# GpSimd multiplies two of the rows that VectorE adds: a two-layer graph attention kernel, layer 1

## The chip, the core and the metric

The kernel runs on 1 core of one Trainium2 chip. The metric is the device time of one execution in microseconds (us), the median of several runs. Engines are named as in the profile: PE is TensorE (PEld its weight loads), DVE is VectorE, ACT is ScalarE, POOL is GpSimd, SP is SyncE.

## The reference, cut to what matters

A graph of 10,000 nodes with 170,000 directed edges (80,000 random ones in both directions and a loop at each node). Two graph attention layers with a residual product, each followed by layer norms. Layer 1 has 4 heads of 256 columns, so a row of it has 1024; layer 2 has one head of 768.

```python
def gat_conv(x, edge_index, W, a_src, a_dst, bias, heads, out_ch, concat):
    ...
    xl = (x @ W).reshape(n, heads, out_ch)
    alpha_src = jnp.einsum('nhc,hc->nh', xl, a_src)
    alpha_dst = jnp.einsum('nhc,hc->nh', xl, a_dst)
    e = jax.nn.leaky_relu(alpha_src[src] + alpha_dst[dst], 0.2)
    m = jax.ops.segment_max(e, dst, num_segments=n)
    e = jnp.exp(e - m[dst])
    s = jax.ops.segment_sum(e, dst, num_segments=n)
    alpha = e / (s[dst] + 1e-16)
    msg = xl[src] * alpha[:, :, None]
    out = jax.ops.segment_sum(msg, dst, num_segments=n)
    ...
h = gat_conv(x, edge_index, W1, a_src1, a_dst1, b1, HEADS, HID, True)
h = jax.nn.relu(layer_norm(h, g1, be1)) + (h0 @ Wr1 + br1)
h1 = h
h = gat_conv(h, edge_index, W2, a_src2, a_dst2, b2, 1, OUT_DIM, False)
h = layer_norm(h, g2, be2) + (h1 @ Wr2 + br2)
x = _layernorm(x + h)
```

## The kernel before, in words

There are three parts. First (up to about 740 us) all rows `x @ W1` are computed and written to a table in HBM, each with its logit parts behind its 1024 columns, while the edges are sorted. Then layer 1 (about 766 to 3080 us) and layer 2 (to the end) go over 79 tiles of 128 nodes. The nodes are sorted by the number of their edges, so that a tile needs `SLOTS[t]` rows, one for each edge of its node with the most edges. The order of the tiles, `TURNS`, lets the sizes of layer 1 rise from 7 to 41 rows and fall again to 9.

Row k of a tile is fetched by one indirect DMA, which GpSimd issues (L470): 128 partitions, each its own table row of 4132 bytes. The rows go into a ring of 31 places (`RING1`); `ring.fetch` asks for a row when the one 31 before it has been used, so each gather waits for whoever used that place last.

The weighted sum over a tile's rows is shared between three engines by row:

- The first `on_pe(t)` rows: ScalarE multiplies the row in its place by the weights, one ACTIVATE for each of 4 heads (L558), and TensorE adds it up with an identity matmul (L931), for tile t + 1 while tile t is under way. The sum is the accumulator in PSUM.
- "Weighed" rows (`weighed(t)` of them, spread over the tile): VectorE multiplies and adds at once, four 128x256 instructions (L569).
- "Shared" rows (the rest): ScalarE multiplies (L558), VectorE adds one 128x1024 instruction (L565).

`PARTED` is 22: tiles with 22 rows or more are done in several parts, with a running maximum, and are not touched by the change. `FEW` is 11.

All engines work through their instructions in the order in which the program gives them. Within the loop over the rows k of tile t, `multiplied(k + 1 + LEAD)` puts ScalarE's multiplies four rows ahead of VectorE's add. At k = `soon - 2` (`soon` is n - 3, or n - 4 where the next tile has more than two rows on TensorE) GpSimd adds up the next tile's logits (L937 to L942); two rows later VectorE takes leaky ReLU and maximum (L194, L950, L953), ScalarE the exponent (L954), and a row after that VectorE divides by the sum (L974 to L976), after which ScalarE can begin with the next tile's rows. The last add of a tile is followed by the normalisation on VectorE (L580, L582, L594, L596, L1084), whose standard deviation comes from ScalarE (L584, L585). TensorE multiplies the tile's x by Wr1 (L177) and the normalised rows by W2 (L1156). SP issues the stores of x, of h1 and of layer 2's table row.

Of the kernel before, what the change touches and what calls it, by code (L numbers as in the profile page):

```python
# [32 lines left out]
OP = mybir.AluOpType  # L33
# [23 lines left out]
PARTED = 22  # L57
FEW = 11
# [26 lines left out]
def gnn_kernel(ctx, tc, x, x_cols, src, dst, src_col, dst_col, W1, a_src1, a_dst1, b1, g1, be1, Wr1, br1,  # L85
               W2, a_src2, a_dst2, b2, g2, be2, Wr2, br2, out, n_edges):
    nc = tc.nc
    N, D0 = out.shape
    H1, DH1 = a_src1.shape
# [10 lines left out]
    SLOTS = CAPS  # L100
# [3 lines left out]
    FIRST, TOTAL = [0] * NT, 0  # L104
# [449 lines left out]
    def multiply(row, e, dh):  # L554

        for h in range(e.shape[1]):
            s = slice(h * dh, (h + 1) * dh)
            nc.scalar.activation(row[:, s], row[:, s], AF.Copy, scale=e[:, h:h + 1])  # L558

    def weigh(acc, row, e, dh, first=None, shared=False):  # L560


        if shared:
            c = e.shape[1] * dh
            nc.vector.tensor_add(acc[:, :c], acc[:, :c], row[:, :c])  # L565
            return
        for h in range(e.shape[1]):
            s = slice(h * dh, (h + 1) * dh)
            nc.vector.scalar_tensor_tensor(acc[:, s], row[:, s], e[:, h:h + 1],  # L569
                                           (acc if first is None else first)[:, s], op0=OP.mult, op1=OP.add)  # L570
# [41 lines left out]
    with tc.tile_pool(name="w1", bufs=1) as w1p, tc.tile_pool(name="l1", bufs=2) as io, \  # L612
# [63 lines left out]
        def new_row():  # L676
            return io.tile([P, R1], F32, name="row", bufs=4)
# [57 lines left out]
        for t in range(NT % 2):  # L735
            xT, row = xTs.pop(t), new_row()
# [94 lines left out]
    SLOTS, FIRST = [SLOTS[t] for t in TURNS], [FIRST[t] for t in TURNS]  # L831
# [35 lines left out]
    def ordered_layer1(mem):  # L867
        nc.scalar.add_instruction(mybir.InstLoadActFuncSet(name=nc.get_next_instruction_name(), act_func_set_id=6, engine=nc.scalar.engine))
        with tc.tile_pool(name="b1", bufs=1) as pool, tc.tile_pool(name="small1", bufs=2) as small, \
# [3 lines left out]
            ring = Ring(table1, RING1, {}, [mem.rearrange("p (k n) -> p k n", n=R1)])  # L873
# [35 lines left out]

            accs = [ps_acc.tile([P, 2 * BANK], F32, name=f"acc{i}") for i in range(2)]  # L910

            def on_pe(t):


                n = SLOTS[t]
                if n <= FEW + 1:
                    return int(n > FEW)
                return min((n - FEW) // 2 + (n > 18 and n % 2 == 0), ON_PE1)

            def later_on_pe(t):  # L920

                return min(max((SLOTS[t] - 20) // 2, 1), ON_PE1 - 2)
# [34 lines left out]
            def weights_of(t):  # L957

                n, m, at = SLOTS[t], on_pe(t), FIRST[t]
                cuts = cuts_of(t)  # L960
                ad = ring.slot(at)[:, C1:C1 + H1]
# [53 lines left out]
            def cuts_of(t):  # L1015

                n = SLOTS[t]
                groups = 1 if n < PARTED else -(-2 * n // ring.size)
                size = 8 if groups == 2 else (n - 5) // groups
                return [0] + [n - size * g for g in range(groups - 1, -1, -1)]  # L1020

            def by_vector(t, k):
                lo = max(c for c in cuts_of(t)[:-1] if c <= k)
                return k - lo >= (later_on_pe(t) if lo else on_pe(t))

            def weighed(t):

                return sum(SLOTS[t] >= n for n in (0, 0, 17, 19))

            def shared(t, k):  # L1030
                i = k - on_pe(t)
                if len(cuts_of(t)) > 2:
                    return by_vector(t, k) and i % (SHARE - 1) > 0
                w = weighed(t)
                return by_vector(t, k) and i * w % (SLOTS[t] - on_pe(t)) >= w

            last = None
            full = None
# [29 lines left out]
            for t in range(NT + 1):  # L1068
                live, events = t < NT, []
                n = SLOTS[t] if live else 0  # L1070
                first = done = on_pe(t) if live else 0
                cuts = cuts_of(t) if live else []
                moves = []

                def started():

                    r_before, means = last
                    return r_before, means, deviation(small, pieces(means[:, :C1], BANK))

                def normalised(r_before, means, stats):  # L1080

                    h = pool.tile([P, C1], F32, name="h")
                    scaled(h, [means[:, :C1]], stats, g1_b, be1_b)
                    nc.vector.scalar_tensor_tensor(h, h, 0.0, r_before[:, :C1], op0=OP.max, op1=OP.add)  # L1084
                    return h

                early = live and last and not ready
                if early:
# [6 lines left out]
                    h, moves = normalised(*started()), []  # L1095
# [6 lines left out]
                def row_of(k):  # L1102
                    lo = max(c for c in es if c <= k)
                    return es[lo][0][:, k - lo], es[lo][1] if k == lo else None

                def multiplied(upto):
                    nonlocal done
                    while done < min(upto, n):
                        if shared(t, done):
                            multiply(ring.slot(FIRST[t] + done), row_of(done)[0], DH1)  # L1110
                        done += 1

# [13 lines left out]
                if live and t and not early and not turned:  # L1126
                    xT, moves = from_x(t)
                turned, turn = [], live and 0 < t < NT - 1 and len(cuts) == 2
                multiplied(first + 2)
                if last and not early:  # L1130
                    h = normalised(*norm)
                if not live:
                    begun = next(begin)
                for move in moves:
                    move()
                multiplied(first + LEAD)
                if last:
                    hT = pool.tile([P, K1, P], F32, name="hT")
# [39 lines left out]
                def due(k):  # L1178
                    while events and events[0][0] <= k:
                        events.pop(0)[1]()  # L1180
# [10 lines left out]
                for k in range(n):  # L1191
                    if k + 3 * LEAD + 2 in cuts[1:-1]:
                        next(later)
                    if k + 2 * LEAD + 2 in cuts[1:-1]:
                        next(later)
                    if k + 2 * LEAD in cuts[1:-1]:
                        lo, es_lo = next(later)
                        es[lo] = es_lo
                    multiplied(k + 1 + LEAD)
                    if k == soon - 2:  # L1200
                        next(ahead, None)
                    if soon <= k < soon + 2:
                        ready += itertools.islice(ahead, 1)
                    if k + 2 in cuts[1:-1]:
                        next(later)
                    weights, fade = row_of(k)
                    if fade is not None:
                        for h in range(H1):
                            s = slice(h * DH1, (h + 1) * DH1)
                            nc.vector.scalar_tensor_tensor(acc[:, s], acc[:, s], fade[:, h:h + 1], ring.slot(FIRST[t] + k)[:, s],  # L1210
                                                           op0=OP.mult, op1=OP.add)
                    if not k and by_vector(t, k):
                        for h in range(H1):
                            s = slice(h * DH1, (h + 1) * DH1)
                            nc.vector.tensor_scalar(acc[:, s], ring.slot(FIRST[t])[:, s], weights[:, h:h + 1], None,
                                                    op0=OP.mult)
                    elif by_vector(t, k):
                        weigh(acc, ring.slot(FIRST[t] + k), weights, DH1, shared=shared(t, k))
                    if t:
                        ring.fetch(min(FIRST[t] + k + 1 + ring.size, upto[t][k >= soon - 2] if t in upto else TOTAL))  # L1220
                    due(k)
# [453 lines left out]
    with tc.If(all_fits > 0) as fit:  # L1675
        with tc.tile_pool(name="rows", bufs=1) as rows_pool:
            mem = rows_pool.tile([P, RING1 * R1], F32, name="ring")
            ordered_layer2(mem, ordered_layer1(mem))
# [49 lines left out]
```

## Time and profile before

| | us |
|---|---|
| median of 3 runs | 4923.9 (4920.7 to 4933.22) |
| profiled execution | 4928.81, span 4926.9 |

| Engine | busy us | share of the span |
|---|---|---|
| PE | 4379.8 | 89% |
| DVE | 4216.4 | 86% |
| ACT | 3291.0 | 67% |
| POOL | 3444.1 | 70% |

The profile is one execution, taken by the hardware profiler. A row of a group gives line, engine, operation, what is written and read, count, busy time, the mean in ns of one instruction, and the idle time of the engine before them with what ended it; "issue" stands for idle time in which the engine waited for nothing that the profile shows. A row in order of time gives start, length, engine, line and operation; like instructions that follow each other are merged with their count. Busy time of PE is modelled, and each matmul of 512 columns stands as two records.

### The profile page before, as it was taken

The page shows a single profiled execution, that of the slowest core. Times are in us where ns is not written, and L with a number is a line of the kernel's source. Part 1 is how long each engine was busy: PE and PEld are TensorE (multiplying, and loading weights), DVE is VectorE, ACT ScalarE, POOL GpSimd, SP SyncE. Part 2 cuts the span into 40 slices and gives each one's busy share as a digit, 9 for nine tenths or more (in the row PEclk, how much of TensorE's full clock was granted, in tenths as well). Part 3 has the DMA queues.
Part 4 walks back from the last instruction along what each step waited for, and adds up shares of the span by engine and source line. Part 5 has one row for each costly group of instructions (what it writes and reads, how often), then busy time and mean ns, then how long its engine had stood idle before and what let it go on. Part 6 is the DMA issues. An engine that isn't in the chain of part 4 may idle for free. (4 is left out here: it accounts for less than half of the span.)

```text
span 4926.9 us, 52519 instructions
## 1 busy us (share of the span) xinstructions
PE 4379.8 (89%) x12262; PEld 2264.3 (46%) x12262; DVE 4216.4 (86%) x5935; ACT 3291.0 (67%) x8969; POOL 3444.1 (70%) x3722
## 2 busy tenths in 40 slices
PE   9999998999999997899999999788787887787884
PEld 4443444554545543445444545444444444444442
DVE  7887897899999998898999998588887888888887
ACT  5753445899999998889999987344444444444443
POOL 6876766666777777777776664477777777777774
PEclk9999999999999999999999999889898898998987
DMA  4323438999999998999999996799999999999996
GB/s 162 124 104 129 103 108 330 352 359 370 379 378 391 401 384 296 361 370 389 389 376 375 368 356 244 285 369 372 360 375 369 369 369 366 370 368 365 370 367 224
DMA packets 433415, 1588.03 MB, mean 322 GB/s; under 512 B 77207, under 2 KB 82135, under 8 KB 433094
## 3 DMA queue, kind: packets, MB, share of 16 engines
q0 software_dynamic: 321040, 1283.72, 70.3%
q1 hardware_dynamic: 99490, 269.38, 14.6%
q10 hardware_dynamic: 12564, 31.47, 2.0%
q8 instruction: 101, 1.65, 0.1%
q14 instruction: 220, 1.80, 0.1%
HBM read 1426.26 MB, written 177.29 MB: 325 GB/s over the span
## 5 line engine op out<-in xcount | busy, mean ns | idle before, releaser
L470 POOL DMA_INDIRECT ring<-table,slots x2663 | 2646.9, 994 | 1123.5 <-issue 366.7
L558 ACT ACTIVATE ring<-ring,e 128x256 f32<-128x256 f32 x4468 | 1823.4, 502 | 71.8 <-DVE e L976 51.7
L569 DVE SCALAR_TENSOR_TENSOR acc<-ring,e,acc 128x256 f32<-128x256 f32 (+1 forms) x1915 | 1426.3, 745 | 81.0 <-PE acc L931 25.2
L565 DVE TENSOR_TENSOR acc<-acc,ring 128x1024 f32<-128x1024 f32 x869 | 1069.9, 1231 | 70.7 <-ACT ring L558 12.1
L1156 PE MATMUL half<-w,hT 128*128 128x512 f32 (+1 forms) x2528 | 841.2, 486 | 0.0
L177 PE MATMUL big<-wr,xT 128*128 128x512 f32 x1896 | 829.4, 594 | 0.5 <-ACT xT L892 0.5
L1348 PE MATMUL big<-wr,w 128*128 128x512 f32 (+1 forms) x2464 | 810.6, 487 | 13.6 <-ACT w L1354 12.5
L1156 PEld LDWEIGHTS half<-w,hT 128*128 128x128 f32 x2528 | 472.8, 189 | 341.6 <-issue 295.4
L1348 PEld LDWEIGHTS big<-wr,w 128*128 128x128 f32 x2464 | 468.6, 190 | 344.2 <-issue 298.6
L177 PEld LDWEIGHTS big<-wr,xT 128*128 128x128 f32 x1896 | 355.2, 191 | 417.9 <-issue 417.1
L931 PE MATMUL acc<-ring,ident 128*128 128x512 f32 x992 | 460.1, 612 | 71.1 <-ACT ring L558 50.4
L1314 PE MATMUL sums<-ring,diagonals 128*128 128x512 f32 x740 | 304.3, 569 | 182.9 <-ACT diagonals L1311 167.9
L1314 PE MATMUL sums<-ring,w 128*128 128x512 f32 x736 | 291.3, 553 | 172.4 <-ACT w L1311 172.4
L541 ACT ACTIVATE e<-e,least 128x19 f32<-128x19 f32 (+14 forms) x82 | 25.3, 308 | 614.1 <-DVE least L537 592.3
L690 ACT ACTIVATE scr<-scr 128x256 f32<-128x256 f32 x624 | 250.5, 403 | 160.5 <-DVE scr L683 156.3
L931 PEld LDWEIGHTS acc<-ring,ident 128*128 128x128 f32 x992 | 187.8, 194 | 305.6 <-issue 145.8
L1314 PEld LDWEIGHTS sums<-ring,diagonals 128*128 128x128 f32 x740 | 161.8, 223 | 320.7 <-ACT diagonals L1311 193.6
L630 PE MATMUL one<-wr,mixed 128*128 128x512 f32 x702 | 307.6, 592 | 0.0
L1314 PEld LDWEIGHTS sums<-ring,w 128*128 128x128 f32 x736 | 157.4, 218 | 302.0 <-ACT w L1311 183.3
L695 POOL TENSOR_TENSOR row<-row,none 128x1024 f32<-128x1024 f32 x69 | 168.2, 2438 | 115.1 <-DVE scr L683 45.7
L1362 ACT ACTIVATE spare<-acc 128x768 f32<-128x768 f32 x158 | 126.8, 802 | 167.6 <-DVE acc L1376 92.6
L630 PE MATMUL one<-w,xT 128*128 128x512 f32 x492 | 227.0, 598 | 10.8 <-DMA w<-in_W_dram 5.6
(236 smaller groups left out, 4697.7 us busy)
## 6 DMA issues: line engine op xcount, KB each, us to landing
ring<-table,slots POOLq DMA_INDIRECT x2663, 6.6
h_d<-hT SPq DMA_DIRECT2D x79, 512.0 KB, 8.5
table<-row SPq DMA_DIRECT2D x78, 516.0 KB, 3.2
w<-h_d SPq DMA_DIRECT2D x77, 512.0 KB, 8.5
table<-row SPq DMA_DIRECT2D x79, 385.0 KB, 6.3
ring<-table SPq DMA_DIRECT2D x79, 385.0 KB, 6.5
w<-x_d SPq DMA_DIRECT2D x79, 384.0 KB, 6.8
x_d<-xt SPq DMA_DIRECT2D x77, 384.0 KB, 6.4
```

Source lines behind the costliest of these rows:

```text
L177: nc.tensor.matmul(p[:, c:e], aT[:, j, :], w[:, j, c:e], start=(j == 0), stop=(j == k - 1))
L470: nc.gpsimd.indirect_dma_start(out=to, out_offset=None, in_=table, in_offset=bass.IndirectOffsetOnAxis(ap=index, axis=0), **more)
L558: nc.scalar.activation(row[:, s], row[:, s], AF.Copy, scale=e[:, h:h + 1])
L565: nc.vector.tensor_add(acc[:, :c], acc[:, :c], row[:, :c])
L569: nc.vector.scalar_tensor_tensor(acc[:, s], row[:, s], e[:, h:h + 1], (acc if first is None else first)[:, s], op0=OP.mult, op1=OP.add)
L630: nc.tensor.matmul(p, aT[:, j, :], w[:, j, :], start=(start and j == 0), stop=(j == k - 1), skip_group_check=True)
L690: nc.scalar.activation(m[:, s], m[:, s], AF.Copy, accum_out=row[:, C1 + i * H1 + h:C1 + i * H1 + h + 1])
L695: engine.tensor_add(row[:, lo:hi], row[:, lo:hi], b1_b[:, lo:hi])
L931: nc.tensor.matmul(acc[:, c:c + BANK], ident, ring.slot(q + k)[:, c:c + BANK], start=(k == 0), stop=(k == m - 1))
L1156: nc.tensor.matmul(q, hT[:, j, :], w2[:, j, c:c + q.shape[1]], start=(j == 0), stop=(j == K1 - 1))
L1314: nc.tensor.matmul(to[:, c:d], diagonal, ring.slot(at + k)[:, c:d], start=(k == n - m), stop=(k == n - 1))
L1348: nc.tensor.matmul(r[:, c:d], hT[:, j, :], wr2[:, j, c:d], start=(j == 0), stop=(j == K1 - 1))
```

## The change

Tiles of layer 1 with 13 to 21 rows (`helped`; the first tile of the order is left out) share their rows in another way. Of each, the last two shared rows are multiplied by GpSimd, four instructions of 128x256 a row, in place in the ring, and not by ScalarE. They stand in GpSimd's queue ahead of the gathers that belong to rows 1 and 3 of the tile. VectorE adds these rows as it adds the other shared ones. VectorE weighs no row at 13 to 16 rows (two before), one at 17 and 18 (three before), two at 19 to 21 (four before). TensorE sums (n - 12) // 2 rows, at least one, which is one fewer than before at 15, 17, 19, 20 and 21 rows.

```diff
+            def helped(t):
+
+                return 0 < t and FEW + 2 <= SLOTS[t] < PARTED
+
             def on_pe(t):
                 n = SLOTS[t]
+                if helped(t):
+                    return max((n - FEW - 1) // 2, 1)
                 if n <= FEW + 1:
                     return int(n > FEW)
                 return min((n - FEW) // 2 + (n > 18 and n % 2 == 0), ON_PE1)
...
             def weighed(t):
 
-                return sum(SLOTS[t] >= n for n in (0, 0, 17, 19))
+                return sum(SLOTS[t] >= n for n in ((17, 19) if helped(t) else (0, 0, 17, 19)))
...
+            def by_pool(t):
+
+                return [k for k in range(SLOTS[t]) if shared(t, k)][-2:] if helped(t) else []
...
                 cuts = cuts_of(t) if live else []
+                given = by_pool(t) if live else []
...
                     while done < min(upto, n):
-                        if shared(t, done):
+                        if shared(t, done) and done not in given:
                             multiply(ring.slot(FIRST[t] + done), row_of(done)[0], DH1)
                         done += 1
...
                     multiplied(k + 1 + LEAD)
+                    if k in (1, 3) and given:
+                        row, weights = ring.slot(FIRST[t] + given[k // 2]), row_of(given[k // 2])[0]
+                        for h in range(H1):
+                            s = slice(h * DH1, (h + 1) * DH1)
+                            nc.gpsimd.tensor_scalar(row[:, s], row[:, s], weights[:, h:h + 1], None, op0=OP.mult)
                     if k == soon - 2:
                         next(ahead, None)
```

## The prediction

> **What bounds the kernel now.** First the page (span, the engines' busy times, the costliest groups), then the busy times per stretch, then the order of time inside two tiles.
>
> ```profile
> span 4926.9 us, 52519 instructions
> PE 4379.8 (89%) x12262; PEld 2264.3 (46%) x12262; DVE 4216.4 (86%) x5935; ACT 3291.0 (67%) x8969; POOL 3444.1 (70%) x3722
> L470 POOL DMA_INDIRECT ring<-table,slots x2663 | 2646.9, 994 | 1123.5 <-issue 366.7
> L565 DVE TENSOR_TENSOR acc<-acc,ring 128x1024 f32<-128x1024 f32 x869 | 1069.9, 1231 | 70.7 <-ACT ring L558 12.1
> ```
>
> The whole-run shares hide what counts. Layer 1's tiles of 13 to 21 rows stand twice in the run, on a rising and a falling flank. The rows below are the falling flank, one stretch for each size from 21 down to 13 (2, 3, 3, 4, 3, 4, 4, 3 and 2 tiles), each cut at the last normalising step (L1084). Columns: stretch, its length, then busy time (and instructions) of PE, PEld, DVE, ACT, POOL, the granted clock, DMA share, GB/s.
>
> ```profile
> 2198.80:2265.20 66.40, 64.18 (x190) 32.42 (x189) 58.34 (x80) 61.56 (x158) 48.54 (x60) 1.00 1.00 376
> 2265.20:2356.80 91.60, 91.60 (x269) 47.03 (x268) 83.44 (x118) 87.75 (x225) 68.70 (x81) 1.00 1.02 401
> 2356.80:2446.10 89.30, 86.22 (x255) 44.13 (x254) 83.13 (x117) 81.25 (x208) 64.48 (x76) 1.00 1.02 389
> 2446.10:2562.80 116.70, 110.13 (x324) 56.27 (x323) 108.14 (x145) 109.53 (x281) 83.02 (x101) 0.99 1.00 377
> 2562.80:2647.80 85.00, 83.43 (x248) 42.58 (x247) 77.35 (x105) 76.37 (x196) 58.59 (x69) 1.00 1.01 382
> 2647.80:2757.70 109.90, 105.80 (x314) 54.24 (x313) 100.05 (x128) 103.24 (x266) 72.17 (x90) 0.98 0.98 363
> 2757.70:2860.30 102.60, 102.22 (x311) 53.41 (x309) 95.11 (x124) 95.33 (x245) 68.04 (x86) 1.00 0.99 372
> 2860.30:2936.50 76.20, 72.29 (x223) 38.16 (x222) 71.23 (x94) 68.59 (x175) 48.48 (x63) 1.00 0.97 352
> 2936.50:2985.60 49.10, 47.81 (x149) 25.51 (x148) 44.93 (x60) 42.27 (x108) 29.61 (x36) 1.00 0.98 354
> ```
>
> TensorE, VectorE and ScalarE are all between 86% and 100% here: three bounds lie within a few per cent of each other, so relief of one pays only up to the next. GpSimd looks free at 60 to 75%. It is not: its gathers do not follow one another without a gap. These are its rows at the end of a 20-row tile.
>
> ```profile
> 1608.33 0.99 POOL L470 DMA_INDIRECT ring<-table,slots  x1 [0.30 <-issue]
> 1609.32 0.12 POOL L937 MEMSET e<- 128x4 f32 x1
> 1609.39 0.36 POOL L939 TENSOR_TENSOR e<-ring 128x68 f32<-128x68 f32 x1
> 1611.69 1.07 POOL L470 DMA_INDIRECT ring<-table,slots  x1 [0.61 <-DVE e L953]
> 1615.73 0.99 POOL L470 DMA_INDIRECT ring<-table,slots  x1 [0.30 <-issue]
> 1621.11 1.85 POOL L470 DMA_INDIRECT ring<-table,slots  x1 [0.31 <-issue]
> ```
>
> A gather is 0.99 us long, but 0.30 us of idle time stands before each, also where it waits for nothing ("issue"): the pace is 1.29 us. A compute step follows a gather with no gap (1608.33 + 0.99 = 1609.32), and after the logits the gap is 0.61. So GpSimd's demand for a tile of n rows is its busy time, 0.30 for each of n + 1 gathers (one is x's), and 0.30 after the logits. For 20 rows: 68.70 / 3 = 22.9, plus 6.3, plus 0.3, makes 29.5 us of the 91.60 / 3 = 30.5 us that a tile takes. What is left over for GpSimd, by the same arithmetic, for 13 to 21 rows: 5.2, 4.4, 3.5, 4.0, 3.1, 2.4, 2.0, 1.0 and 2.0 us.
>
> **The change, part by part.** It touches 57 tiles (5, 6, 7, 8, 7, 8, 6, 6 and 4 of the sizes 13 to 21, layer 1 without its first turn). By the two helpers that count rows, VectorE weighs two rows fewer in each (114 rows). TensorE sums one row fewer at 15, 17, 19, 20 and 21 rows (30 tiles). VectorE adds two rows more at 13, 14, 16, 18 and three more at the others (144 rows). ScalarE multiplies as many rows as before: 30 fewer for TensorE, 144 more for VectorE, 114 given to GpSimd. GpSimd gets 2 x 4 multiplies of 128x256 a tile, 456 in all. No transfer, no SP instruction and no ScalarE queue entry is moved past another kind; the multiplies are put into GpSimd's queue ahead of the gathers of rows 1 and 3.
>
> The prices of VectorE and ScalarE come from a 15-row tile, ScalarE first, in order of time (start, length):
>
> ```profile
> 2807.51 4.90 ACT L558 ACTIVATE ring<-ring,e 128x256 f32<-128x256 f32 x12
> 2812.30 0.57 ACT L892 COPY hT<-half 128x512 f32<-128x512 f32 x1
> 2812.77 1.71 ACT L558 ACTIVATE ring<-ring,e 128x256 f32<-128x256 f32 x4
> 2814.84 11.28 ACT L558 ACTIVATE ring<-ring,e 128x256 f32<-128x256 f32 x28
> 2826.36 0.25 ACT L954 ACTIVATE e<-e 128x60 f32<-128x60 f32 x1 [0.24 <-DVE e L953]
> 2820.72 2.06 DVE L569 SCALAR_TENSOR_TENSOR acc<-ring,e,acc 128x256 f32<-128x256 f32 x4
> 2822.87 2.56 DVE L565 TENSOR_TENSOR acc<-acc,ring 128x1024 f32<-128x1024 f32 x2
> 2825.50 0.22 DVE L194 SCALAR_TENSOR_TENSOR e<-e 128x60 f32<-128x60 f32 x1
> 2826.18 1.22 DVE L565 TENSOR_TENSOR acc<-acc,ring 128x1024 f32<-128x1024 f32 x1
> 2827.96 2.49 DVE L565 TENSOR_TENSOR acc<-acc,ring 128x1024 f32<-128x1024 f32 x2
> 2830.49 0.70 DVE L580 BATCH_NORM_STATS2 st<-acc 128x6 f32<-128x512 f32 x1
> ```
>
> - VectorE: a weighed row takes 2822.87 - 2820.72 = 2.15 us, an added one (2825.50 - 2822.87) / 2 = 1.31. Two weighed for two added saves 1.7 us a tile, two for three saves 0.4.
> - TensorE: one row is four of the matmuls at L931, whose pace I take from the 24 of a tile's product at L177, 10.46 / 24 = 0.43 us (quoted below), so 1.7 us less in 30 tiles.
> - ScalarE: 1.61 us a row (11.28 for 7). This is slower than VectorE's add. Until now each weighed row, which needs no ScalarE, let it catch up; now two of these are gone and its rows end earlier in the tile, with GpSimd's two behind them. For 15 rows: today ScalarE does 11 of VectorE's rows from 2807.51 on; it will do 12, and 2807.51 + 12 x 1.61 + 0.93 (two hT copies) = 2827.8. VectorE then adds row 11 (ready 2826.2), does the logit steps (0.68, from 2825.50 to 2826.18), and starts row 12 at 2828.2 instead of 2826.18. Behind it stand the same three adds and the normalisation. That is +2.0 to +2.1 us although VectorE has less to do. The same subtraction gives 0, +1.0, +0.7 and +0.2 at 13, 14, 16 and 17. At 18 to 21, where ScalarE has more rows' lead and VectorE or TensorE held the end, it gives -1.2, -0.2, -0.8 and -0.6. Over the 57 tiles this is about +10 us: without any GpSimd cost the change is a wash.
> - GpSimd's multiply is not in the trace. The nearest rows:
>
> ```profile
> L702 POOL TENSOR_TENSOR mixed<-xT 128x384 f32<-128x384 f32 x20 | 22.2, 1110 | 0.5 <-PE one L630 0.5
> L695 POOL TENSOR_TENSOR row<-row,none 128x1024 f32<-128x1024 f32 x69 | 168.2, 2438 | 115.1 <-DVE scr L683 45.7 <-issue 30.6 <-DVE have L416 24.0
> L941 POOL TENSOR_SCALAR slots<-ring 128x2 int32<-128x2 f32 x4 | 1.1, 262 | 0.3
> L941 POOL TENSOR_SCALAR slots<-ring 128x18 int32<-128x18 f32 x5 | 1.6, 323 | 0.4
> L942 POOL MEMSET ring<- 128x25 f32 x12 | 1.5, 123 | 0.7
> L942 POOL MEMSET ring<- 128x90 f32 x5 | 0.9, 183 | 0.3
> 2811.35 10.46 PE L177 MATMUL big<-wr,xT 128*128 128x512 f32 x24
> ```
>
> A two-operand step grows by (2438 - 1110) / 640 = 2.08 ns an element; with one tensor operand I take half, 1.04, on the fixed 0.26 us of the small tensor-scalar: 0.26 + 256 x 1.04 ns = 0.53 us, so 8 x 0.53 = 4.2 us a tile. Low end: a memset, which reads nothing, carried on to 256 columns by its own slope, 0.183 + 166 x (183 - 123) / 65 ns = 0.34 us, 2.7 us a tile. High end: the small tensor-scalar's own slope, (323 - 262) / 16 = 3.8 ns, is from strided single elements and would give 1.2; the two-operand slope gives 0.79. I hold 0.34 to 0.85 for likely.
>
> The Trainium skill (GPSIMD Engine Reference, section 3.1) has a simple one-operand body at about 1.03 cycles an element of a 1.2 GHz clock; as an estimate that is 0.22 us on the same 0.26, 3.8 us a tile, and the sum below would be +77 instead of +90. No row here shows it.
>
> Sum for GpSimd: 4.2 us against the spare time above overruns by 0.7, 0.2, 1.1, 1.8, 2.3, 3.2 and 2.2 us at 15 to 21 rows; below 15 it fits. Per size the larger of this and ScalarE's tail holds, since both lie on one chain: gathers and multiplies, logits, VectorE's logit steps, weights, ScalarE's rows. 6 x 1.0 + 7 x 2.1 + 8 x 0.7 + 7 x 1.1 + 8 x 1.8 + 6 x 2.3 + 6 x 3.2 + 4 x 2.2 = **+90 us**.
>
> **Waits.** The multiply itself waits for little: its row has landed (the logits read it) and its weights are a tile's tail old. Behind it stand the gathers and then the next tile's logits at L939, for which VectorE's L194 waits; that wait should grow. The two rows' results are needed some ten adds (13 us) later, so VectorE does not wait for the multiply; were that cover gone, up to 2.1 us a row would show. The gathers start later, but GpSimd then sets the pace for their use too, so landing stays hidden.
>
> **Against the executions.** The profiled one took 4928.8 us (span 4926.9), 5 us above the median 4923.9. 4923.9 + 90 = **5014 us**.
>
> **Rivals.**
> 1. The aim is met: GpSimd and ScalarE's tail hide, and TensorE's idle time in the stretches at 13, 14, 16 and 18 rows (0.65, 1.3, 1.0, 1.6 us a tile) is what VectorE's 1.7 us can win, 32 us, plus 0.4 in 30 tiles: -44, **4880 us**. For it: VectorE is nearly full at 14 and 18 rows. Against: at 20 rows GpSimd has 1.0 us left, and eight fixed parts alone are 2.1. It decides if the multiply, in effect, costs under 0.2 us and ScalarE runs ahead of VectorE.
> 2. GpSimd's share is hidden, ScalarE's tail is not: +10, **4934 us**, no change. It needs the same small multiply.
> 3. A cheap multiply of 0.34 us: overruns only at 18 to 21 rows, 0.3, 0.7, 1.7 and 0.7: +47, **4971 us**.
> 4. A dear multiply, 0.73 to 0.85: the overrun reaches all sizes, +156 to +210, **5080 to 5134 us**.
> 5. A held port. The gather at 1621.11 took 1.85 us rather than 0.99, while VectorE ran the step below, two operands of which are in SBUF; VectorE's adds have the accumulator in PSUM.
>
> ```profile
> 1620.82 1.28 DVE L596 SCALAR_TENSOR_TENSOR h<-h,sd,norm 128x1024 f32<-128x1024 f32 x1
> ```
>
> If each tile's first multiply falls on this step, either waits: up to 0.86 us in 57 tiles, +49 on the sum, **5063 us**. The Trainium skill (SBUF — State Buffer, section Who interferes with whom) says such a VectorE step and a GpSimd step that reads SBUF exclude each other for a whole instruction; this gather agrees. By the section the adds would not be held.
>
> **How the numbers follow.** Chances: the forecast with a multiply of about 0.4 to 0.65 (4980 to 5050, its own range) 0.50; rival 5, 0.10; rival 4, 0.12; rival 3, 0.12; rival 2, 0.07; rival 1, 0.09. A measurement tells about 0.3%, 15 us, from no change. So faster 0.09, same 0.07, slower 0.84. From 4925 to 5110 the range takes in rivals 2, 3, 5 and most of 4 and leaves out rival 1 and the dearest multiplies, about 0.17.
>
> **What would show it.** In the profile of the changed kernel: a GpSimd tensor-scalar group, ring from ring, 456 times, near 0.53 us each; GpSimd's gathers at 18 to 21 rows all with the bare 0.30 before them; VectorE's L194 waiting for GpSimd's logits by 2 to 3 us a tile at those sizes, and its adds waiting for ScalarE's rows at 14 and 15; stretches of 20 rows near 33.7 us a tile and of 15 near 27.7. It is wrong if the multiply is near 0.2 us, if it runs beside the gathers' 0.30 gaps, or if ScalarE's rows are never late.

## The result, and the profile after

The changed kernel takes 5281.47 us (median of 6 runs), the kernel before 4929.47 us on the same chip (6 runs): a ratio of 1.0721, interval [1.071, 1.0732]. That is 352 us slower; 90 us were forecast. The profiled execution took 5287.69 us.

The page of the kernel after: span, busy times, and the groups that answer to those quoted of before (line, engine, operation, tile, count, then busy us and mean ns of one, then idle time ahead of it and what ended it). The edit moved L939 to L945, L954 to L960 and L931 to L937; L194, L470, L558, L565 and L596 kept their numbers.

```profile
span 5285.8 us, 52439 instructions
PE 4445.5 (84%) x12142; PEld 2287.2 (43%) x12142; DVE 4173.6 (79%) x5623; ACT 3293.7 (62%) x8969; POOL 3861.7 (73%) x4178
L565 DVE TENSOR_TENSOR acc<-acc,ring 128x1024 f32<-128x1024 f32 x1013 | 1247.3, 1231 | 145.8 <-ACT ring L558 77.0
L1215 POOL TENSOR_SCALAR ring<-ring,e 128x256 f32<-128x256 f32 x456 | 424.8, 945 | 4.5
L194 DVE SCALAR_TENSOR_TENSOR e<-e 128x56 f32<-128x56 f32 (+25 forms) x174 | 34.8, 200 | 352.9 <-POOL e L945 349.6
L960 ACT ACTIVATE e<-e 128x56 f32<-128x56 f32 (+12 forms) x92 | 23.2, 252 | 430.3 <-DVE e L959 423.2
```

The multiply (L1215) has a mean of 945 ns, not 530. VectorE's busy time fell by 43 us, as meant; its share fell by more than that because the span grew. The idle time in L194's row says why: VectorE now stands idle for 349.6 us ahead of its logit step, until GpSimd's logits (L945) are there. Before, this was 45.7 us:

```profile
L194 DVE SCALAR_TENSOR_TENSOR e<-e 128x56 f32<-128x56 f32 (+25 forms) x174 | 34.5, 198 | 49.9 <-POOL e L939 45.7 <-DVE e L533 0.2
```

So this wait grew by 304 us, most of the 352 us lost; counted in the 57 changed tiles alone, it grew from 10 to 317 us. ScalarE's exponent (L960) waits behind it.

The stretches of the falling flank, again cut at the last normalising step, for 21, 20, 16 and 15 rows (2, 3, 4 and 4 tiles; columns as in the prediction):

```profile
2379.90:2457.40 77.50, 61.69 (x170) 30.92 (x171) 57.80 (x70) 61.51 (x157) 63.31 (x75) 0.91 0.88 320
2457.40:2568.90 111.50, 90.68 (x251) 44.79 (x250) 83.13 (x102) 86.15 (x221) 89.52 (x104) 0.93 0.89 326
...
2933.40:3071.40 138.00, 112.48 (x314) 56.55 (x312) 94.64 (x105) 101.95 (x262) 102.69 (x123) 0.90 0.82 294
3071.40:3194.30 122.90, 104.07 (x296) 53.26 (x296) 94.16 (x105) 97.40 (x249) 100.00 (x120) 0.94 0.86 309
```

No engine's busy time fills a stretch any longer: at 20 rows GpSimd has the second most, 89.52 of 111.50 us, behind PE's 90.68. Its rows in time show that it is nonetheless the bound there. One 20-row tile, from the last gathers of the tile before to the logits; the fence begins and ends with VectorE's steps beside it:

```profile
1741.99 1.32 DVE L596 SCALAR_TENSOR_TENSOR h<-h,sd,norm 128x1024 f32<-128x1024 f32 x1 [0.39 <-ACT sd L585]
1741.38 0.99 POOL L470 DMA_INDIRECT ring<-table,slots  x1 [0.30 <-issue]
1742.41 4.41 POOL L1215 TENSOR_SCALAR ring<-ring,e 128x256 f32<-128x256 f32 x4
1746.99 1.06 POOL L470 DMA_INDIRECT ring<-table,slots  x1 [0.17 <-issue]
1748.35 1.01 POOL L470 DMA_INDIRECT ring<-table,slots  x1 [0.30 <-issue]
1749.40 3.64 POOL L1215 TENSOR_SCALAR ring<-ring,e 128x256 f32<-128x256 f32 x4
1753.20 1.06 POOL L470 DMA_INDIRECT ring<-table,slots  x1 [0.16 <-issue]
...
1768.59 0.36 POOL L945 TENSOR_TENSOR e<-ring 128x68 f32<-128x68 f32 x1
1769.77 0.24 DVE L194 SCALAR_TENSOR_TENSOR e<-e 128x80 f32<-128x80 f32 x1 [7.49 <-POOL e L945]
```

Nothing but the bare gap of the pace (about 0.3 us ahead of a gather) stands between GpSimd's steps, the logits come as late as its queue makes them, and VectorE waits 7.49 us. The first group of four meets L596 and takes 4.41 us instead of 3.64.

At 16 rows the queue is not full. One tile of that size:

```profile
2965.40 0.99 POOL L470 DMA_INDIRECT ring<-table,slots  x1 [0.30 <-DVE st L580]
2969.85 0.99 POOL L470 DMA_INDIRECT ring<-table,slots  x1 [3.46 <-ACT ring L558]
2970.89 3.65 POOL L1215 TENSOR_SCALAR ring<-ring,e 128x256 f32<-128x256 f32 x4
2974.71 1.06 POOL L470 DMA_INDIRECT ring<-table,slots  x1 [0.16 <-issue]
2976.07 1.02 POOL L470 DMA_INDIRECT ring<-table,slots  x1 [0.30 <-issue]
2977.12 3.63 POOL L1215 TENSOR_SCALAR ring<-ring,e 128x256 f32<-128x256 f32 x4
2980.92 1.06 POOL L470 DMA_INDIRECT ring<-table,slots  x1 [0.17 <-issue]
...
2992.49 0.34 POOL L945 TENSOR_TENSOR e<-ring 128x64 f32<-128x64 f32 x1
2992.87 0.23 DVE L194 SCALAR_TENSOR_TENSOR e<-e 128x64 f32<-128x64 f32 x1 [6.30 <-POOL e L945]
```

Here GpSimd waits 3.46 us at 2969.85 for the place of row 0 in the ring, and only then comes to the first multiply. From there to the logits there is no gap but the pace's. So part of what I had counted as spare lies ahead of the multiplies, where they cannot use it. The wait ends with one of ScalarE's multiplies (L558), and by the program these need the weights from the logits that GpSimd made in the tile before: the wait is a link of the loop of logits, weights, freed place, gather and logits again.

Mean time of a tile by size, both flanks, from one last normalising step to the next:

| Rows | 13 | 14 | 15 | 16 | 17 | 18 | 19 | 20 | 21 |
|---|---|---|---|---|---|---|---|---|---|
| before | 24.9 | 25.5 | 25.9 | 27.4 | 28.2 | 29.4 | 29.7 | 30.8 | 32.3 |
| after | 29.2 | 29.6 | 30.7 | 34.3 | 35.8 | 36.2 | 37.4 | 37.2 | 38.8 |
| more by | 4.3 | 4.1 | 4.8 | 6.9 | 7.6 | 6.8 | 7.7 | 6.4 | 6.5 |
| 7.5 less the spare time of the prediction | 2.3 | 3.1 | 4.0 | 3.5 | 4.4 | 5.1 | 5.5 | 6.5 | 5.5 |
| after: wait ahead of row 0's gather, above 0.30 | 1.8 | 0.4 | 0.7 | 3.2 | 3.5 | 2.3 | 1.9 | 0.0 | 0.0 |

The 57 tiles together went from 1602 to 1957 us, so all of the loss is in them (the tiles of 22 rows and more: 483 and 484 us). The fourth row is my own queue step with the measured price, 8 x 0.945 = 7.56 us, put as 7.5; over the 57 tiles it makes 252 us. At 20 rows, where the queue is full, it meets the measurement; at 16 and 17 rows it is 3 us short. The last row is the idle time, in the trace of after, ahead of the gather that precedes the first multiply. It makes 96 us over the 57 tiles, and the two rows together make 348 of the 355 us. This is a count of where GpSimd still idles; whether work could have used that time is tested by the run early. Between the first multiply and the next logits a gather stands idle longer than the pace's gap in only one of the 57 tiles, by 0.39 us.

### The profile page after: what moved, and what is told of

It is laid out like the page before. It is cut to its first block, busy times and chain, and to the rows that moved or that the text cites. A ratio compares the mean times of both kernels' runs of the same rounds, so it can differ in the third digit from the quotient of the medians.

```text
span 5285.8 us, 52439 instructions
## 1 busy us (share of the span) xinstructions
PE 4445.5 (84%) x12142; PEld 2287.2 (43%) x12142; DVE 4173.6 (79%) x5623; ACT 3293.7 (62%) x8969; POOL 3861.7 (73%) x4178
## 5 line engine op out<-in xcount | busy, mean ns | idle before, releaser
L470 POOL DMA_INDIRECT ring<-table,slots x2663 | 2636.9, 990 | 1060.2 <-issue 417.3
L558 ACT ACTIVATE ring<-ring,e 128x256 f32<-128x256 f32 x4468 | 1824.0, 501 | 78.3 <-DVE e L982 60.8
L565 DVE TENSOR_TENSOR acc<-acc,ring 128x1024 f32<-128x1024 f32 x1013 | 1247.3, 1231 | 145.8 <-ACT ring L558 77.0
L569 DVE SCALAR_TENSOR_TENSOR acc<-ring,e,acc 128x768 f32<-128x768 f32 (+1 forms) x1459 | 1203.4, 825 | 102.3 <-PE acc L937 60.9
L177 PE MATMUL big<-wr,xT 128*128 128x512 f32 x1896 | 850.4, 606 | 0.3 <-ACT xT L892 0.3
L937 PE MATMUL acc<-ring,ident 128*128 128x512 f32 x872 | 489.7, 717 | 310.8 <-ACT xT L892 211.9
L937 PEld LDWEIGHTS acc<-ring,ident 128*128 128x128 f32 x872 | 192.7, 230 | 570.8 <-ACT xT L892 228.5
L1215 POOL TENSOR_SCALAR ring<-ring,e 128x256 f32<-128x256 f32 x456 | 424.8, 945 | 4.5
L194 DVE SCALAR_TENSOR_TENSOR e<-e 128x56 f32<-128x56 f32 (+25 forms) x174 | 34.8, 200 | 352.9 <-POOL e L945 349.6
L960 ACT ACTIVATE e<-e 128x56 f32<-128x56 f32 (+12 forms) x92 | 23.2, 252 | 430.3 <-DVE e L959 423.2
```

The costliest lines, as they stand in the source:

```text
L177: nc.tensor.matmul(p[:, c:e], aT[:, j, :], w[:, j, c:e], start=(j == 0), stop=(j == k - 1))
L470: nc.gpsimd.indirect_dma_start(out=to, out_offset=None, in_=table, in_offset=bass.IndirectOffsetOnAxis(ap=index, axis=0), **more)
L937: nc.tensor.matmul(acc[:, c:c + BANK], ident, ring.slot(q + k)[:, c:c + BANK], start=(k == 0), stop=(k == m - 1))
L1215: nc.gpsimd.tensor_scalar(row[:, s], row[:, s], weights[:, h:h + 1], None, op0=OP.mult)
```

## The experiments

The kernels no_multiplies, multiplies_only, early, one_instruction, early_four and earlier_one ran on a chip on which the kernel before takes about 5412 us; the changed kernel itself was not run there. Ratios alone mislead here. That chip's extra time lies mostly in layer 2, which the change leaves alone: from the last normalising step of layer 1 to the end its traces take 2253 to 2264 us, those of before and after on the other chips 1827 and 1830. So the same loss in layer 1 is a smaller share of the whole there. The text therefore gives, beside each ratio, the time above before on the same chip, from the two medians; for the change it is 352 us. The tiles of layer 1 with fewer than 13 and more than 21 rows take 4 to 6% longer there too, so these differences may be off by some per cent.

**The change again**, beside kernels of the second group: 5279.48 us, ratio 1.0714 [1.0696, 1.0731].

> The changed kernel once more, as the measure for the others of this group on their chip: 1.072 of the time before by either theory.

That is 355 us above before. It is the yardstick for that group, and says that the result is steady.

**The price of the multiply by itself.** Groups of six GpSimd instructions behind the end of the before kernel's work (each loop is put on one line here):

```
+            a, b, unit = spare[:, :DH1], spare[:, DH1:2 * DH1], loops[:, 0:1]
+            for _ in range(6): nc.gpsimd.tensor_scalar(a, a, unit, None, op0=OP.mult)
+            for _ in range(6): nc.gpsimd.tensor_scalar(a, a, 1.0, None, op0=OP.mult)
+            for _ in range(6): nc.gpsimd.tensor_copy(a, b)
+            for _ in range(6): nc.gpsimd.tensor_tensor(a, a, b, op=OP.mult)
+            for _ in range(6): nc.gpsimd.tensor_tensor(a, b, unit.to_broadcast([P, DH1]), op=OP.mult)
+            for _ in range(6): nc.gpsimd.tensor_scalar(spare[:, :2 * DH1], spare[:, :2 * DH1], unit, None, op0=OP.mult)
+            for _ in range(6): nc.gpsimd.tensor_scalar(a[:, :P], a[:, :P], unit, None, op0=OP.mult)
```

> The kernel before with seven groups of six GpSimd instructions behind its last tile, where no other engine works: tensor-scalar by a per-partition operand 128x256, the same by a constant, copy, two-operand multiply, multiply by a spread column, tensor-scalar 128x512 and 128x128. Theory of the elements (about 3.4 ns each, whatever the second operand): per-partition and constant both 0.92 us, 512 columns 1.8, 128 columns 0.48. Theory of the operand (fetching the per-partition operand costs a fixed 0.4 us): constant 0.5, 512 columns 1.2, 128 columns 0.8.

Its groups on GpSimd (L1469 and L1471 are the 512 and 128 columns):

```profile
L1469 POOL TENSOR_SCALAR spare<-spare,loops 128x512 f32<-128x512 f32 x6 | 9.4, 1562 | 0.6
L1459 POOL TENSOR_SCALAR spare<-spare,loops 128x256 f32<-128x256 f32 x6 | 5.6, 932 | 0.5
L1461 POOL TENSOR_SCALAR spare<-spare 128x256 f32<-128x256 f32 x6 | 5.1, 847 | 0.5
L1465 POOL TENSOR_TENSOR spare<-spare 128x256 f32<-128x256 f32 x6 | 4.3, 722 | 0.5
L1467 POOL TENSOR_TENSOR spare<-spare,loops 128x256 f32<-128x256 f32 x6 | 3.7, 612 | 0.5
L1471 POOL TENSOR_SCALAR spare<-spare,loops 128x128 f32<-128x128 f32 x6 | 3.6, 602 | 0.6
L1463 POOL COPY spare<-spare 128x256 f32<-128x256 f32 x6 | 2.4, 399 | 0.4
```

The tensor-scalar grows by (1562 - 602) / 384 = 2.5 ns a column and has a fixed part of 0.28 us. It makes little difference whether the scalar is a column or a constant (932 and 847 ns), which speaks against the theory of the operand; that of the elements had the slope too high and the fixed part too low. The tensor-scalar is dearer than the two-operand multiply (722), and the two-operand form with the weight's column spread out is cheaper still (612). My assumption that a step with one tensor operand grows half as fast as one with two is refuted: here it costs more.

**Sharing without the multiplies, and multiplies without the sharing.**

The first takes these lines out of the changed kernel, the second puts a multiply by a column of ones (`unit`) at the same places into the kernel before:

```
-                    if k in (1, 3) and given:
-                        row, weights = ring.slot(FIRST[t] + given[k // 2]), row_of(given[k // 2])[0]
-                        for h in range(H1):
-                            s = slice(h * DH1, (h + 1) * DH1)
-                            nc.gpsimd.tensor_scalar(row[:, s], row[:, s], weights[:, h:h + 1], None, op0=OP.mult)
```

```
+                    if k in (1, 3) and live and helped(t):
+                        row = ring.slot(FIRST[t] + n - 2 + k // 2)
+                        for h in range(H1):
+                            s = slice(h * DH1, (h + 1) * DH1)
+                            nc.gpsimd.tensor_scalar(row[:, s], row[:, s], unit[:, h:h + 1], None, op0=OP.mult)
```

> Leaves out GpSimd's 456 multiplies, so two rows of each of the 57 tiles are added unweighted; the new sharing between TensorE, VectorE and ScalarE stays. Queue theory (the multiplies stand in GpSimd's queue between the gather of row 0 and the next tile's logits, and cost what they take there; the sharing is nearly neutral): about the time before, 4915 to 4945 us. Sharing theory (the loss beyond 8 x 0.93 us of occupancy, some 105 us, comes from ScalarE's rows that VectorE now waits for): 5030 us.

> The kernel before with its own sharing, and with GpSimd multiplying the last two rows of each of the 57 tiles by 1.0 at the changed kernel's places (ahead of the gathers of rows 1 and 3), before ScalarE weighs them. Queue theory: nearly the whole loss, 5240 to 5290 us. Sharing theory: occupancy alone, 5170 us.

Without the multiplies: 5443.79 us, ratio 1.0053 [1.0032, 1.0073], 32 us above before. Multiplies alone: 5774.86 us, ratio 1.0684 [1.0651, 1.0716], 363 us above before. So GpSimd's multiplies alone make the whole loss, and the sharing by itself costs about 32 us, where the step on ScalarE's tail had +10. VectorE's idle time ahead of L194 follows the multiplies: 50 us in before, 48 without them, 354 with them alone, 353 in after. By size the tiles of no_multiplies take 25.6, 26.4, 27.8, 28.3, 28.5 and 29.4 us at 13 to 18 rows: +0.7, +0.9, +1.9, +0.9, +0.3 and 0 against before. The step had 0, +1.0, +2.1, +0.7, +0.2 and -1.2. The gains that it had for 18 to 21 rows did not come. Whether the 1.7 and 2.8 us more at 19 and 21 rows belong to the sharing or to that chip stays open, since no trace of before was taken there.

**Both multiplies ahead of row 0's gather**, in the same four instructions a row.

```
-                    if k in (1, 3) and given:
+                    if not k and given:
+                        for g in given:
+                            row, weights = ring.slot(FIRST[t] + g), row_of(g)[0]
...
```

> The changed kernel with both rows' multiplies ahead of the gather of row 0 instead of behind those of rows 0 and 2. Queue theory: the 3.5 us for which GpSimd waits for row 0's place at 16 and 17 rows (15 tiles) are used, and something less at other sizes: 50 to 100 us faster than the changed kernel, 5180 to 5230 us. If that idle time costs nothing: 5281 us, no change.

5686.21 us, ratio 1.0514 [1.0481, 1.0547], 274 us above before. The wait for row 0's place is now used, and the loss falls by 78 us, within the 50 to 100 expected. The relief is where the wait was: the tiles of 16 and 17 rows are 2.4 and 2.7 us shorter than in after, those of 20 and 21 rows within 0.3. Part of what that gained went back into a meeting with VectorE's L596. Its group of multiplies, and then, in order of time, a run of eight and the L596 beside it:

```profile
L1216 POOL TENSOR_SCALAR ring<-ring,e 128x256 f32<-128x256 f32 x456 | 457.4, 1016 | 2.3
```

```profile
2406.90 8.30 POOL L1216 TENSOR_SCALAR ring<-ring,e 128x256 f32<-128x256 f32 x8
2407.80 1.28 DVE L596 SCALAR_TENSOR_TENSOR h<-h,sd,norm 128x1024 f32<-128x1024 f32 x1 [0.39 <-ACT ring L558]
```

The mean rose from 945 to 1016 ns, 32 us over 456. L596, which begins 0.90 us into the run, still takes 1.28 us: here GpSimd gives way. They meet so in 54 of the 57 tiles; the run of eight has a median of 8.01 us there, and of 7.26 in the three others.

**One instruction a row in place of four**, at the places of the change.

```
-                        for h in range(H1):
-                            s = slice(h * DH1, (h + 1) * DH1)
-                            nc.gpsimd.tensor_scalar(row[:, s], row[:, s], weights[:, h:h + 1], None, op0=OP.mult)
+                        row = row[:, :C1].rearrange("p (h c) -> p h c", h=H1)
+                        nc.gpsimd.tensor_tensor(row, row, weights[:, :, None].to_broadcast([P, H1, DH1]), op=OP.mult)
```

> The changed kernel, each row multiplied by one two-operand GpSimd instruction of 128x1024 (the weights spread over 256 columns each) instead of four tensor-scalars of 128x256. Price theory (fixed part and slope of the two-operand rows before, 2.44 us for 1024 columns, against 4 x 0.92): 1.2 us a row, 2.4 us a tile, about 140 us faster than the changed kernel, 5140 us. If GpSimd's time is set by the elements and not by the form: no change, 5281 us.

Its group:

```profile
L1214 POOL TENSOR_TENSOR ring<-ring,e 128x1024 f32<-128x1024 f32 x114 | 218.6, 1918 | 2.6
```

5559.55 us, ratio 1.0276 [1.0253, 1.03], 148 us above before. A row costs 1.92 us instead of 3.65, which is 3.5 us a tile, about 200 us over 57 tiles; the loss fell by 352 - 148 = 204 us. The price is paid one to one. This is the strongest single proof of the queue theory. (The expectation had the saving too small, 2.4 us a tile.)

**Both: one instruction a row, ahead of row 0's gather** (early with the `tensor_tensor` above).

> The changed kernel with both means together: one 128x1024 multiply a row (1.92 us) and both rows ahead of the gather of row 0. Queue theory (what is not hidden in the wait for row 0's place costs its length): 3.8 us a tile, of which 3.5 are hidden at 16 and 17 rows and about 1 to 2 elsewhere: 1.010 to 1.020 of the time before. If the early place only helped because the four-part multiply was long: 1.027, as with one instruction alone.

5060.79 us, ratio 1.0273 [1.0256, 1.029], 136 us above before, where one_instruction had 148. Being early gained next to nothing on top. The reason is L596 (its durations between 1000 and 3300 us as min/median/max ns, and one instance beside the multiplies):

```profile
L596 DVE SCALAR_TENSOR_TENSOR h<-h,sd,norm x71: 1283/3821/4334, 1002.9 to 3233.1; 128x1024 f32<-128x1024 f32 x71
```

```profile
2624.58 3.75 POOL L1215 TENSOR_TENSOR ring<-ring,e 128x1024 f32<-128x1024 f32 x2
2625.09 4.33 DVE L596 SCALAR_TENSOR_TENSOR h<-h,sd,norm 128x1024 f32<-128x1024 f32 x1
```

L596 begins 0.51 us into the pair and ends at 2629.42, 1.09 us behind the pair's end. In all 54 tiles where the pair began first, L596 ends 1.09 us behind the pair's end, wherever it began (0.51 to 2.69 us into the pair). So it is not slowed but held, until about the end of both multiplies, and VectorE loses 2.5 us in most tiles. The tensor-scalar did not do that to it.

**Shorter pieces**: early_one with each row's multiply in four.

```
-                            row = row[:, :C1].rearrange("p (h c) -> p h c", h=H1)
-                            nc.gpsimd.tensor_tensor(row, row, weights[:, :, None].to_broadcast([P, H1, DH1]), op=OP.mult)
+                            for h in range(H1):
+                                part = row[:, h * DH1:(h + 1) * DH1]
+                                nc.gpsimd.tensor_tensor(part, part, weights[:, h:h + 1].to_broadcast([P, DH1]), op=OP.mult)
```

> The kernel early_one (both multiplies ahead of row 0's gather, one 128x1024 two-operand instruction each) with each multiply cut into four two-operand instructions of 128x256, each with a spread column of weights (0.61 us each in the row of six alone, so 2.6 us a row with gaps, 5.2 a tile against 3.75). In early_one VectorE's step L596 took a median of 3.82 us instead of 1.28 between 1000 and 3300 us: it begins about 0.5 us behind the pair of multiplies and ends with them. Theory of the held step (L596 cannot begin its reads while a two-operand GpSimd instruction runs, and waits for that instruction's end): with short pieces L596's median falls to 1.9 to 2.5 us, VectorE gets back 1.3 to 1.9 us a tile where it is the bound, GpSimd gives up 1.5 us where it is: ratio to before 1.012 to 1.030. Rival (L596 waits for the whole run of multiplies, however cut, or is slowed by their reads): L596's median 4 us or more, ratio 1.035 to 1.05.

5595.12 us, ratio 1.0342 [1.0311, 1.0373], 181 us above before, and L596 is as long as in early_one:

```profile
L596 DVE SCALAR_TENSOR_TENSOR h<-h,sd,norm x69: 1283/3789/4582, 1017.5 to 3281.2; 128x1024 f32<-128x1024 f32 x69
```

```profile
2437.84 5.58 POOL L1216 TENSOR_TENSOR ring<-ring,e 128x256 f32<-128x256 f32 x8
2438.73 4.22 DVE L596 SCALAR_TENSOR_TENSOR h<-h,sd,norm 128x1024 f32<-128x1024 f32 x1 [0.39 <-ACT ring L558]
```

My theory that L596 waits for the instruction under way falls: a piece is 0.6 us, and L596 was held for 4.22 - 1.28 = 2.9 us. It waits through a run of multiplies that follow one another without a gap, however cut. It ends 0.47 us ahead of the run's end in 47 of the 51 tiles in which they meet, and the eighth piece then takes longer (median 1.58 us, the others 0.60 to 0.63): it got in at the last piece. Why there is not settled. The rival's 4 us and 1.035 were missed by a little on the low side.

**Two instructions, out of L596's way**: behind the final weights of the tile ahead, before the last gathers of the tile before (the same `tensor_tensor` a row, ahead of the step's `ring.fetch`).

```
-                    if not k and given:
-                        for g in given:
...
+                    if k == soon + 1 and live and helped(t + 1):
+                        for g in by_pool(t + 1):
+                            row, weights = ring.slot(FIRST[t + 1] + g), ready[0][0][0][:, g]
...
```

> The kernel early_one with the two 128x1024 multiplies moved ahead once more: behind the final weights of the tile ahead and before the last two or three gathers of the tile before (instead of behind them all, ahead of row 0's gather), so that they are over when VectorE reaches L596 and GpSimd spends its wait for row 0's place on the gathers that they delayed. Theory that place and price alone made the loss: L596 is back at 1.28 us, GpSimd's wait ahead of row 0's gather goes from 3.5 us to under 1.5, and what is left is ScalarE's tail at 14, 15 and 17 rows (my step for it: +10 us in all): ratio to before 0.998 to 1.010. Rival (the sharing itself, VectorE's two weighed rows fewer and TensorE's row fewer, leaves ScalarE the bound and no more can be had than without the multiplies, which gave 1.005; and the gathers behind the multiplies come late): ratio 1.010 to 1.025, with VectorE idle for rows.

5506.15 us, ratio 1.019 [1.0156, 1.0223], 92 us above before. L596's durations, and GpSimd around one pair, that of a 19-row tile:

```profile
L596 DVE SCALAR_TENSOR_TENSOR h<-h,sd,norm x71: 1283/1285/3544, 1012.0 to 3235.0; 128x1024 f32<-128x1024 f32 x71
```

```profile
2452.49 3.76 POOL L1234 TENSOR_TENSOR ring<-ring,e 128x1024 f32<-128x1024 f32 x2
2456.41 1.02 POOL L470 DMA_INDIRECT ring<-table,slots  x1 [0.16 <-ACT sd L585]
2457.74 1.43 POOL L470 DMA_INDIRECT ring<-table,slots  x1 [0.30 <-issue]
2459.48 0.99 POOL L470 DMA_INDIRECT ring<-table,slots  x1 [0.30 <-issue]
```

L596's median is back at 1285 ns (in 17 tiles it still meets the pair), and the wait ahead of row 0's gather is gone here, as expected; 44 us of early_one's 136 came back. But the ratio is the rival's. At 14 to 17 rows the tiles take 26.4, 27.5, 28.3 and 29.4 us; without any multiply they took 26.4, 27.8, 28.3 and 28.5. So there, up to 16 rows, GpSimd is hidden at last, and what is left is the sharing's own cost. VectorE is idle 2 to 3.5 us a tile at these sizes (gaps of over 0.15 us counted). At 18 rows and more two multiplies are still 3.8 us against a spare time of 1.0 to 2.4, by the prediction's count.

**A small dose.** In before, at 13, 14, 16 and 18 rows alone, one weighed row becomes a shared one, and GpSimd multiplies one row with one instruction, ahead of the last gather of the tile before.

```
+            def helped(t):
+                return 1 < t < NT and SLOTS[t] in (13, 14, 16, 18)
-                return sum(SLOTS[t] >= n for n in (0, 0, 17, 19))
+                return sum(SLOTS[t] >= n for n in ((0, 17, 19) if helped(t) else (0, 0, 17, 19)))
+                    if k == n - 1 and live and helped(t + 1):
+                        for g in by_pool(t + 1):
...
```

> The kernel before with one change at 13, 14, 16 and 18 rows alone (27 tiles), where VectorE and not TensorE held the end: one weighed row fewer, and the last shared row multiplied by GpSimd with one 128x1024 instruction, ahead of the last gather of the tile before, so that it ends before row 0's place comes free. Queue theory: VectorE saves 2.15 - 1.31 = 0.84 us a tile, 23 us in all, 0.995 to 0.997 of the time before. If VectorE waits for ScalarE's rows or for the logits instead, or the normalising step at L596 is held by the multiply: 1.000 or a little over.

4928.26 us, ratio 1.0007 [0.9998, 1.0017]: no gain. VectorE is idle 1.1 to 1.5 us a tile at these sizes, where it was idle 0.1 to 1.0 in before (counted in the same way); about half or more of its relief of 0.84 us a tile turned into idle time. In the one profiled execution the tiles of 13, 16 and 18 rows are 0.3 to 0.4 us shorter, and this does not show in the medians. No version that ran beats the kernel before.

## Why the prediction was right or wrong, point by point

- **The sign, the place and the mechanism** were right: GpSimd's queue overruns, VectorE waits for the logits at L194, and the loss is in the 57 tiles, though also in those of 13 and 14 rows, which were forecast to fit. The size, 352 against 90 us, was far outside the range. Two steps of the sum failed, the multiply's price and the spare time.
- **The multiply's price was mis-sized**, 0.53 forecast, 0.945 us measured (least 0.914). With it the same formula gives 252 us instead of 90: 162 of the 262 us missed. The step was "with one tensor operand I take half" of the two-operand slope of 2.08 ns; prices shows 2.5 ns a column for the tensor-scalar, more than the whole of it. I had the better row: the small tensor-scalar, 3.8 ns an element, which I set aside as strided and left out of the likely range. Its slope was half as much again as the measured one; the assumed 1.04 was less than half of it. The estimate from the Trainium skill (GPSIMD Engine Reference, section 3.1), 0.22 + 0.26 us, does not agree with prices either, 0.93 us. one_instruction shows that the price is what counts: 1.7 us off a row took 204 of the 352 us away.
- **The spare time was taken as usable wherever it lay**; this is the rest, about 100 us, 1.8 us a tile, and the wait ahead of row 0's gather in after makes 96 us. The trace of before already had the wait ahead of row 0's gather, here in a 16-row tile:

```profile
2671.54 0.99 POOL L470 DMA_INDIRECT ring<-table,slots  x1 [0.30 <-PE half L1156]
2674.53 0.99 POOL L470 DMA_INDIRECT ring<-table,slots  x1 [2.00 <-ACT ring L558]
```

  Work placed behind that gather cannot run in its wait. With all in front of it (early) 78 us came back, although each multiply became 7% longer, which is 32 us.
- **ScalarE's tail** was about right where it was a loss (13 to 17 rows), as no_multiplies and earlier_one show; after itself has it at 15 rows, where VectorE's adds wait 3.2 us a tile for ScalarE's rows. The 15-row tile without a GpSimd cost took 27.5 to 27.8 us, forecast 27.7. The gains at 18 to 21 rows were not seen, so that the whole came to about 32 us, not 10.
- **"The larger of the two counts"** was not tested by itself: with 0.945 us the queue is the larger at all sizes. That no_multiplies and multiplies_only lose 32 + 363 us and the change, with both, 352, speaks for it, but these are two chips.
- **Waits**: L194's wait was put at 2 to 3 us a tile at 18 to 21 rows; it is 7.49 in the 20-row tile shown and 5.7 to 7.3 on average at these sizes. The bare gap at 20 rows is there. The adds wait for ScalarE as said (L565: 77.0 us on L558, before 12.1).
- **Rival 5, the held port**, is real but small in the change: mean less median of the multiply, (945 - 917) x 456 = 13 us, for 49 forecast. There it was the multiply that got longer. That it would be VectorE's step, as in early_one, I had said only as "either waits".
- **Rival 4** (a dear multiply) is the case that came, beyond its upper price of 0.85. Its sum goes by the same spare time: even with 0.945 us it gives 252 us, not 352.

## What to carry to other kernels

Price an instruction that the trace does not have by the same operation on the same engine, however small or odd that row is, and keep its slope inside the range; do not derive it from another operation by counting operands. When an engine issues the gathers in order, look for where in its queue the idle time lies: time ahead of a waiting gather is open only to work that is queued ahead of it. An engine's relief is worth only the distance to the next bound; here relieving VectorE brought nothing, even where the helper's work was nearly hidden (best) or left out (no_multiplies). Where two chips differ in a stage that the change leaves alone, compare the extra microseconds: ratios would have put the gain of early at 2% of the run, about 100 us, where 78 came back.

## What was not expected of the hardware

- GpSimd's multiply of 128x1024 by four spread columns takes 1.92 us, four tensor-scalars of 128x256 3.65 us, for the same result; a copy of 128x256 takes 0.40, the tensor-scalar 0.93.
- Which side is held where a VectorE step with two operands in SBUF (L596) meets GpSimd depends on GpSimd's form. L596 began 0.90 us into a run of tensor-scalars and took 1.28 us, with the run longer; it began 0.51 us into a run of two-operand multiplies and took 4.33. one_instruction has more: where L596 began 0.36 to 0.55 us ahead of a two-operand multiply, while the gather before that was under way, it took 3.35 to 3.55 us; where it began 0.82 us or more ahead, it took 1.28 to 1.34, and the multiply got longer instead. The Trainium skill (SBUF — State Buffer, section Who interferes with whom) says that the order of issue decides and not the shape of the operation, and that the first holds the pair for its whole instruction. The two-operand runs of early_one and early_four agree that the first one holds, but over several instructions in a row (2.9 us over pieces of 0.6). The tensor-scalar runs do not agree, as by their recorded starts they began first and gave way.
